# Forming the sums of two weight matrices two chunks after their loads, adding the last product last, and ending the last pair on VectorE

## The chip, the cores and the metric

The kernel runs on one core of one Trainium2 chip. A core has five engines, each with a queue of its own that it works off in order: TensorE (PE, matmuls; PEld is its weight load), VectorE (DVE), ScalarE (ACT), GpSimd (POOL) and SyncE (SP, which here only issues DMAs). An instruction that waits holds up everything behind it in its own queue. The metric is the device time of one execution in microseconds (us), median of several runs.

## What is computed

The reference takes x of shape (8, 1024, 512), normalizes each row to xn, and adds the product of two branches:

```python
x = L0_attn_x
xn = _layernorm(x, axis=-1)
s = _L0_attn_ref(xn, ...)             # four heads of 128 columns, joined by warboss_w
g = _silu(_L0_ffn_ref(xn, w1, b1, w2, b2))
x = x + s * g
...
h = jax.nn.relu(jnp.einsum('bsd,dw->bsw', x, w1) + b1)   # 512 -> 2048
return jnp.einsum('bsw,wd->bsd', h, w2) + b2             # 2048 -> 512
```

The four heads are a full attention ("local"), an attention in which each row keeps its 102 largest scores ("sparse"), a memory head and a small prediction head. All in float32.

## The kernel before

**Tiles.** For each of 8 batches there are 8 tiles of 128 tokens, in 4 pairs of 256 tokens. The feed-forward branch works on groups of 512 tokens (16 of them) for the first matrix, and on pairs (32) for the second.

**Seven products instead of eight.** Both feed-forward matmuls use a 2x2 block scheme with seven products. The weights are cut into 8 "up" chunks (w1) and 8 "down" chunks (w2); a chunk is a tile `w` of seven slots of 128x256. Three slots are loaded as they stand, a fourth raw block `extra` is loaded beside them, and four slots are sums and differences made on the chip: on DVE for "up", on POOL for "down". Slot order is the order in which PE uses them: slots 0 and 1 of a chunk are loaded ones, slot 2 is the first sum. The finished chunk is also written to a DRAM buffer (`w_up_dram`, `w_down_dram`) and loaded from there ready made every later time. So sums are made only for the first 16 chunks of `order_of_chunks`, in the first group: up 0 to 4, then down 0, up 5, down 1, up 6, down 2, up 7, down 3, and down 4 to 7.

`load_chunk` (line 420) does all of it at once: it takes one of four buffers `w`, issues the loads on SP, then the four sums on DVE or POOL, then the write-back on SP. `feed_forward` (541) calls it for chunk at+3 when PE starts chunk at; `first_tokens` (913) calls it for chunks 0 to 2. `extra` shares a ring of three small buffers, `tmp`, with the memory and prediction heads.

**From products to values.** The seven products of an "up" chunk are copied by ACT from PSUM to `u` (or, after the last "down" chunk of a pair, to `m`), two slots to a copy, the seventh alone. `add_products` (454) adds them up in four POOL instructions, of which the second and third need the seventh product (slot 6). `hidden_units` (491) then has ACT make h = relu; `hidden_sums` (507) makes the four token sums `hs` of a "down" chunk on POOL; `make_gate` (526) adds b2 on POOL and has ACT take the Silu. `token_sums` (475) makes the token sums `t` of a group on POOL.

**The end of a pair.** `finish_pair` (823) multiplies the four heads by warboss_w (matmul po), copies to `o` on ACT, adds the bias on POOL, multiplies by the gate on POOL (`o<-o,m`), adds x (`xr<-xr,o`) on POOL and issues the output DMA from POOL's queue.

**Order of the work.** All of it is written out by a planner in the kernel. `clock` holds a planned time for each engine in columns; `run` (132) picks the first chain of work whose due time has come, by rank, and fills PE's remaining time with the feed-forward matmuls (`filler`). Each helper adds its cost (`on_pool`: 60 + 1.42 columns an element; `on_dve`: 340) and yields a due time. `InOrder` (77) ties every instruction to the one before it on its engine, so that the queues have exactly this order, and makes L85 the line of nearly every instruction in the profile; groups are told apart by their tile names. Selection on DVE is a chain of rounds (`sparse_select`, 687): MAX8 finds the eight largest of a row and MATCH_REPLACE8 strikes them out, 13 rounds a tile. `prepare_stats` (863) loads rows of the next batch as `xs` for their mean and variance; the Sqrt is ACT's (`sd<-ve`).

Names in the profile: ph, f, po, pa, sc, ptp are matmul results (up products, down products, joined heads, attention, scores, transposed probabilities); el and es are the local and sparse exponentials; x_up and x_down are the raw blocks.

Of the kernel before, what the change touches and what calls it, by code (L numbers as in the profile page):

```python
# [15 lines left out]
P = 128  # L16
# [4 lines left out]
def kernel(  # L21
# [163 lines left out]
    def on_dve(op, out, in0, in1):  # L185
        getattr(dve, op)(out, in0, in1)
        on("dve", 340)
# [229 lines left out]
    def halves(ap):  # L417
        return ap.rearrange("p (c n) -> p c n", c=2)

    def load_chunk(at):  # L420
        if at >= len(order_of_chunks):
            return
        kind, n, k = order_of_chunks[at]
        w = sb.tile([P, 7, H], F32, tag="w", name=f"w_{kind}_{n}_{k}", bufs=4)
        w_tiles[kind, n, k] = w
        if n:
            sp.dma_start(out=w, in_=w_dram[kind, k])
            return
        extra = sb.tile([P, H], F32, tag="tmp", name=f"x_{kind}_{k}", bufs=3)
        if kind == "up":  # L430
            for slot, u, h in ((0, 0, 0), (1, 0, 1), (4, 1, 1)):
                sp.dma_start(out=halves(w[:, slot]), in_=w1v[:, h, :, u, k])
            sp.dma_start(out=halves(extra), in_=w1v[:, 0, :, 1, k])
            on_dve("tensor_add", w[:, 5], extra, w[:, 4])
            on_dve("tensor_sub", w[:, 2], w[:, 5], w[:, 0])
            on_dve("tensor_sub", w[:, 3], w[:, 0], extra)
            on_dve("tensor_sub", w[:, 6], w[:, 1], w[:, 2])
        else:
            for slot, h, d in ((0, 0, 0), (1, 1, 0), (6, 1, 1)):
                sp.dma_start(out=w[:, slot], in_=w2v[:, h, k, ts(d, H)])  # L440
            sp.dma_start(out=extra, in_=w2v[:, 0, k, H:])
            on_pool("tensor_sub", w[:, 5], extra, w[:, 0])
            on_pool("tensor_sub", w[:, 2], w[:, 6], w[:, 5])
            on_pool("tensor_sub", w[:, 3], w[:, 6], extra)
            on_pool("tensor_sub", w[:, 4], w[:, 1], w[:, 2])
        sp.dma_start(out=w_dram[kind, k], in_=w)
# [4 lines left out]
    def twice(ap):  # L451
        return ap.unsqueeze(1).to_broadcast([P, 2, H])

    def add_products(m):

        for to, add in (
            (m[:, 1:3], twice(m[:, 0])),
            (m[:, 3:7:3], twice(m[:, 2])),
            (m[:, 6], m[:, 5]),
            (m[:, 4:6], twice(m[:, 3])),  # L460
        ):
            on_pool("tensor_add", to, to, add)
            yield


# [23 lines left out]
        tokens[g] = (b11, b21, t[:, 1], t[:, 2], t[:, 3], t[:, 0], b22)  # L489

    def hidden_units(g, k, m):
        for _ in add_products(m):
            yield pool_is_free
        yield after("pool")
        for j, slots in enumerate(((1, 4), (6, 5))):
            h = sb.tile([P, 2, T], F32, tag=f"h{j}", name=f"h_{2 * g + j}_{k}", bufs=(5, NWC)[j])
            for u in range(2):
                act.activation(h[:, u], m[:, slots[u]], AF.Relu, bias=bcol(k + NWC * u))
                on("act", 280)
            hidden[2 * g + j, k] = h  # L500
        units_made[0] += 1
# [21 lines left out]

    wanted_at = {}

    def make_gate(n, m):
        for _ in add_products(m):
            yield pool_is_free
        gs = [m[:, 1:7:5], m[:, 4:6]]
        for g in gs:  # L530
            on_pool("tensor_add", g, g, b2.rearrange("p (h n) -> p h n", h=2))
            yield pool_is_free
        yield after("pool")
        for g in gs:
            act.activation(g, g, AF.Silu)
            on("act", 360)
        b, p = divmod(n, NP)
        gate[b, p] = gs
        done.add(("gate", b, p))

    def feed_forward():

        sums = []
        for at, (kind, n, k) in enumerate(order_of_chunks):
            if kind == "up":
                wants[0] = lambda: (
                    "constants" in done and n in tokens and units_made[0] > n * NWC + k - 2
                )
            else:
                wants[0] = lambda: (n, k) in operands and wanted_at[n, k] <= clock["pe"] and (  # L550
                    k < NWC - 1 or n == 0 or ("gated", *divmod(n - 1, NP)) in done
                )
            yield 0
            if kind == "down":
                wants[0] = lambda: True
            load_chunk(at + 3)
            w = w_tiles.pop((kind, n, k))
            if kind == "up":
                m = sb.tile([P, 7, T], F32, tag="u", name=f"u_{n}_{k}", bufs=2)
            elif k == NWC - 1:  # L560
                m = sb.tile([P, 7, H], F32, tag="m", name=f"m_{n}")
            for i in range(7):
                if kind == "up":
                    if i % 2 == 0:
                        ps = ring(f"ph_{n}_{k}_{i}", (P, 2, T))
                    for c in range(2):
                        pe.matmul(
                            ps[:, i % 2], halves(w[:, i])[:, c], tokens[n][i][:, c],
                            start=c == 0, stop=c == 1,
                        )  # L570
                        yield T
                else:
                    if i % 2 == 0:
                        if k == 0:
                            sums.append(
                                ps_f.tile([P, 2, H], F32, tag="f", name=f"f_{n}_{i}")
                            )
                        ps = sums[i // 2]

                    pe.matmul(  # L580
                        ps[:, i % 2], operands[n, k][i], w[:, i],
                        start=(k == 0 and i % 2 == 0), stop=(k == NWC - 1),
                        skip_group_check=True,
                    )
                    yield H
                if (i % 2 or i == 6) and (kind == "up" or k == NWC - 1):
                    a = i - i % 2
                    copy(m[:, a : i + 1], ps[:, : i + 1 - a], 180 * (i + 1 - a))
            if kind == "up":
                start(hidden_units(n, k, m), rank=0)  # L590
                if k == NWC - 1:
                    tokens.pop(n)
                    done.add(("up", n))
                    if n + 1 < GROUPS:
                        start(token_sums(n + 1), rank=0)
            else:
                operands.pop((n, k))
                downs_made[0] += 1
                if k == NWC - 1:
                    sums = []  # L600
                    start(make_gate(n, m), rank=2)
# [221 lines left out]
    def finish_pair(b, p):  # L823
        yield needs(*[("head", b, p, h) for h in (LOCAL, 2, 3)])
        if (b, p) != (0, 0):
            yield needs(("out", *divmod(b * NP + p - 1, NP)))
        yield can_borrow(2)
        done.add(("borrowed", b, p))
        both = [borrow(f"wb_{b}_{p}_{k}", warboss_w[ts(k, T), :]) for k in range(2)]
        xs = [load_x("xr", b, 2 * p + j, "xr") for j in range(2)]  # L830
        yield clock["pe"] + AHEAD
        yield needs(("head", b, p, SPARSE))
        yield after("act")
        order = (LOCAL, 2, 3, SPARSE)
        os = []
        for j in range(2):
            ps = ring(f"po_{b}_{p}_{j}", (P, D))
            accumulate(
                ps,
                [heads[b, p, h][:, ts(j, P)] for h in order],  # L840
                [both[h // 2][:, h % 2, :] for h in order],
                D,
            )
            o = sb.tile([P, D], F32, tag="o", name=f"o_{b}_{p}_{j}", bufs=2)
            copy(o, ps, 360)
            on_pool("tensor_add", o, o, wb)
            os.append(o)
            yield pool_is_free
        give_back(2)
        done.add(("joined", b, p))  # L850
        yield needs(("gate", b, p))
        yield after("act")
        for j, o in enumerate(os):
            on_pool("tensor_mul", halves(o), halves(o), gate[b, p][j])
            yield pool_is_free
        done.add(("gated", b, p))
        for j, o in enumerate(os):
            on_pool("tensor_add", xs[j], xs[j], o)
            pool.dma_start(out=out[b, ts(2 * p + j, P), :], in_=xs[j])
        done.add(("out", b, p))  # L860


# [50 lines left out]
    def first_tokens():  # L913
# [6 lines left out]
            due += [ln_apply(0, j, first_x[j]) for j in four]  # L920
        for at in range(3):
            load_chunk(at)
        for g in range(NG):
            for j in range(4 * g, 4 * g + 4):
                yield due[j]
# [93 lines left out]
```

## Time and profile before

| | |
|---|---|
| median of 3 runs | 3025.64 us (3025.1 to 3027.43) |
| the profiled execution's own time | 3025.14 us |
| its span, first to last instruction | 3023.4 us |
| mean granted clock of PE | 0.992 of full speed |
| DMA | 488.29 MB, mean 162 GB/s |
| POOL, u<-u of 128x512, 384 times | 1295 ns each |
| POOL, u<-u of 128x256, 128 times | 741 ns each |
| DVE, a selection round (MAX8, MATCH_REPLACE8) | 1228 and 1208 ns |
| DVE waiting for x_up, in total | 34.6 us, 7 times |
| POOL waiting for x_down, in total | 38.7 us, 6 times |
| ACT, a table load, 132 times | 1283 ns each |

Durations are of one profiled execution. Time outside the span (1.7 us here) belongs to the execution but to no instruction. A timeline row gives start, duration, engine, line, operation and tiles; the bracket at its end gives how long the engine had been idle and what ended that. A float32 matmul appears as two passes, so that 7 products with 2 contraction steps are 28 rows.

### The profile page before, as it was taken

Reading aid. Unit: us, or ns where it says so; the run is one execution under the profiler, and the core shown is the slowest. Engines: PE = TensorE matmul, PEld = TensorE weight load, DVE = VectorE, ACT = ScalarE, POOL = GpSimd, SP = SyncE. Lnnn points to the kernel's source line nnn. Section 1 sums busy time; section 2 is a strip of 40 time slices with the busy share of each in tenths; the row PEclk is TensorE's granted clock in tenths of the full one; section 3 lists DMA queues with packets and bytes.
Section 4 is the critical chain, followed back from the end, with each engine's and each line's share of the span. In section 5 each row is a group of like instructions: output and inputs, shape, how many; then the busy total and the mean of one; then the engine's idle time right before and its main releaser. Section 6 shows DMA issues by size and latency. Waiting matters only on the chain.

```text
span 3023.4 us, 36222 instructions
## 1 busy us (share of the span) xinstructions
PE 2937.0 (97%) x12868; PEld 2313.2 (77%) x12868; DVE 2334.8 (77%) x3158; ACT 1550.0 (51%) x2864; POOL 1656.3 (55%) x2097
## 2 busy tenths in 40 slices
PE   7989999999999999999999999999999999999997
PEld 5767877777777877877777877778878777777786
DVE  6878769787698786987679884899839898778760
ACT  3445544555455644555446564465644556355552
POOL 3475645556346653564636555366653655536566
PEclk9999999999999999999999999999999999999999
DMA  6454444455345453454545534445444544535444
GB/s 183 143 205 157 174 131 148 169 186 186 114 139 192 165 185 133 139 194 142 190 134 174 188 131 169 139 167 188 160 157 153 181 160 149 173 108 181 157 162 152
DMA packets 170052, 488.29 MB, mean 162 GB/s; under 512 B 13966, under 2 KB 76448, under 8 KB 169872
## 3 DMA queue, kind: packets, MB, share of 16 engines
q1 hardware_dynamic: 164256, 468.24, 45.6%
q0 software_dynamic: 5616, 17.74, 1.5%
q8 instruction: 102, 1.67, 0.2%
q14 instruction: 78, 0.64, 0.1%
HBM read 454.47 MB, written 31.46 MB: 161 GB/s over the span
## 4 chain that ended last, share of the span: by engine, by line
PE 85%; DVE 5%; ACT 5%; POOL 2%; DMA 2%; issue 1%; SPq 1%; POOLq 0%; DVEq 0%; ACTq 0%
PE f L85 22%; PE ph L85 21%; PE pa L85 7%; PE po L85 7%; PE sc L85 6%; PE pk L85 4%; PE pv L85 4%; PE ptp L85 3%; PE pq L85 3%; DVE top L85 2%; DVE left L85 2%; PE ppi L85 2%; PE pmp L85 2%; PE pp L85 2%; ACT L85 1%; PE pmo L85 1%
## 5 line engine op out<-in xcount | busy, mean ns | idle before, releaser
L85 POOL TENSOR_TENSOR u<-u 128x512 f32<-128x512 f32 (+1 forms) x512 | 591.7, 1157 | 688.8 <-ACT u L85 669.0
L85 DVE MAX8 top<-left 128x8 f32<-128x1024 f32 x768 | 943.2, 1228 | 26.7
L85 DVE MATCH_REPLACE8 left<-top,left 128x1024 f32<-128x1024 f32 x704 | 850.7, 1208 | 0.0
L85 PE MATMUL f<-w_down,hs 128*128 128x256 f32 x2048 | 542.0, 381 | 2.5 <-ACT m L85 2.2
L85 PE MATMUL ph<-t,w_up 128*128 128x256 f32 x2048 | 487.6, 380 | 2.7 <-ACT u L85 2.4
L85 PEld LDWEIGHTS f<-w_down,hs 128*128 128x128 f32 x2048 | 383.1, 191 | 70.6 <-issue 21.1
L85 PEld LDWEIGHTS ph<-t,w_up 128*128 128x128 f32 x2048 | 383.4, 190 | 66.1 <-issue 15.5
L85 PE MATMUL f<-w_down,h 128*128 128x256 f32 x1536 | 425.3, 382 | 3.6 <-ACT m L85 3.6
L85 PE MATMUL ph<-xnT,w_up 128*128 128x256 f32 x1536 | 389.9, 381 | 0.0
L85 POOL TENSOR_TENSOR hs<-h 128x128 f32<-128x128 f32 x512 | 242.6, 474 | 256.4 <-PE f L85 239.9
L85 ACT COPY u<-ph 128x512 f32<-128x512 f32 (+1 forms) x512 | 264.0, 530 | 167.2 <-PE ph L85 165.8
L85 PEld LDWEIGHTS f<-w_down,h 128*128 128x128 f32 x1536 | 287.6, 191 | 57.2 <-issue 18.1
L85 PEld LDWEIGHTS ph<-xnT,w_up 128*128 128x128 f32 x1536 | 287.4, 191 | 49.7 <-issue 14.7
L85 PE MATMUL sc<-kT,qT 128*128 128x512 f32 x512 | 242.6, 596 | 5.5 <-ACT qT L85 3.2
L85 ACT ACTIVATE h<-u,biasT 128x256 f32<-128x256 f32 x512 | 220.0, 501 | 43.8 <-POOL u L85 43.8
L85 PE MATMUL po<-wb,head 128*128 128x512 f32 x512 | 231.4, 595 | 6.5 <-ACT head L85 6.3
L85 PE MATMUL pa<-pT,v 128*128 128x256 f32 x1024 | 234.4, 383 | 2.4 <-ACT el L85 2.4
L85 PEld LDWEIGHTS pa<-pT,v 128*128 128x128 f32 x1024 | 196.4, 192 | 32.1 <-ACT el L85 3.1
L85 DVE MAX8 top<-s 128x8 f32<-128x1024 f32 x64 | 78.2, 1222 | 164.8 <-ACT s L85 164.7
L85 ACT COPY pT<-ptp 128x512 f32<-128x512 f32 x256 | 149.1, 586 | 96.3 <-PE ptp L85 95.1
L85 POOL TENSOR_TENSOR o<-o,wb 128x512 f32<-128x512 f32 x64 | 81.3, 1271 | 196.5 <-ACT o L85 196.4
L85 POOL TENSOR_TENSOR m<-m 128x512 f32<-128x512 f32 (+1 forms) x128 | 146.9, 1147 | 64.6 <-ACT m L85 60.4
(116 smaller groups left out, 3776.6 us busy)
## 6 DMA issues: line engine op xcount, KB each, us to landing
w_down<-w_down_dram SPq DMA_DIRECT2D x248, 896.0 KB, 4.7
w_up<-w_up_dram SPq DMA_DIRECT2D x120, 896.0 KB, 4.6
wb<-in_L_attn_warboss_w_dram SPq DMA_DIRECT2D x64, 512.0 KB, 6.2
xl<-in_L_attn_x_dram SPq DMA_DIRECT2D x64, 256.0 KB, 4.7
xr<-in_L_attn_x_dram SPq DMA_DIRECT2D x64, 256.0 KB, 3.3
out_dram<-xr POOLq DMA_DIRECT2D x64, 256.0 KB, 3.0
xs<-in_L_attn_x_dram SPq DMA_DIRECT2D x56, 256.0 KB, 4.7
wmp<-_attn_memory_proj_w_dram SPq DMA_DIRECT2D x32, 256.0 KB, 3.0
```

Source lines behind the costliest of these rows:

```text
L85: r = made(*args, **kwargs)
```

## The change

Three things are changed.

1. `load_chunk` keeps only the loads. The sums and the write-back move to a new function `form_chunk`, called for chunk at+1 when PE starts chunk at (where loads are issued for at+3), and once for chunk 0 in `first_tokens`. The raw blocks get seven slices of their own, in the buffer that later holds `m`.
2. `add_products` takes the engine to use, and works in five instructions (two of 512 columns, three of 256) of which only the last needs the seventh product.
3. For the last pair of the last batch, the additions of `make_gate`, the product with the gate and the addition of x are on DVE, and the output DMA is issued on SP. The bias of `o` stays on POOL.

```diff
+    raw = {}
+    raw_blocks = sb.tile([P, 7, H], F32, tag="m", name="raw_blocks")
+
     def load_chunk(at):
...
-        extra = sb.tile([P, H], F32, tag="tmp", name=f"x_{kind}_{k}", bufs=3)
+        extra = raw[kind, k] = raw_blocks[:, at % 7]
         if kind == "up":
             for slot, u, h in ((0, 0, 0), (1, 0, 1), (4, 1, 1)):
                 sp.dma_start(out=halves(w[:, slot]), in_=w1v[:, h, :, u, k])
             sp.dma_start(out=halves(extra), in_=w1v[:, 0, :, 1, k])
+        else:
+            for slot, h, d in ((0, 0, 0), (1, 1, 0), (6, 1, 1)):
+                sp.dma_start(out=w[:, slot], in_=w2v[:, h, k, ts(d, H)])
+            sp.dma_start(out=extra, in_=w2v[:, 0, k, H:])
+
+    def form_chunk(at):
+
+        if at >= len(order_of_chunks) or order_of_chunks[at][1]:
+            return
+        kind, n, k = order_of_chunks[at]
+        w, extra = w_tiles[kind, n, k], raw.pop((kind, k))
+        if kind == "up":
             on_dve("tensor_add", w[:, 5], extra, w[:, 4])
...
-    def add_products(m):
-
-        for to, add in (
+    def add_products(m, add):
+
+        for to, more in (
             (m[:, 1:3], twice(m[:, 0])),
-            (m[:, 3:7:3], twice(m[:, 2])),
-            (m[:, 6], m[:, 5]),
+            (m[:, 3], m[:, 2]),
+            (m[:, 2], m[:, 5]),
             (m[:, 4:6], twice(m[:, 3])),
+            (m[:, 6], m[:, 2]),
         ):
-            on_pool("tensor_add", to, to, add)
+            add("tensor_add", to, to, more)
             yield
...
+    LAST = B * NP - 1
+
     def make_gate(n, m):
-        for _ in add_products(m):
-            yield pool_is_free
+        add, free = (on_dve, lambda: True) if n == LAST else (on_pool, pool_is_free)
+        for _ in add_products(m, add):
+            yield free
...
             load_chunk(at + 3)
+            form_chunk(at + 1)
...
+        late = b * NP + p == LAST
+        op, free = (on_dve, lambda: True) if late else (on_pool, pool_is_free)
         for j, o in enumerate(os):
-            on_pool("tensor_mul", halves(o), halves(o), gate[b, p][j])
-            yield pool_is_free
+            op("tensor_mul", halves(o), halves(o), gate[b, p][j])
+            yield free
         done.add(("gated", b, p))
         for j, o in enumerate(os):
-            on_pool("tensor_add", xs[j], xs[j], o)
-            pool.dma_start(out=out[b, ts(2 * p + j, P), :], in_=xs[j])
+            op("tensor_add", xs[j], xs[j], o)
+            (sp if late else pool).dma_start(out=out[b, ts(2 * p + j, P), :], in_=xs[j])
...
         for at in range(3):
             load_chunk(at)
+        form_chunk(0)
```

More of the change, by code (lines that the diff above doesn't have):

```diff
@@ L438, in load_chunk @@
         else:
-            for slot, h, d in ((0, 0, 0), (1, 1, 0), (6, 1, 1)):
-                sp.dma_start(out=w[:, slot], in_=w2v[:, h, k, ts(d, H)])
-            sp.dma_start(out=extra, in_=w2v[:, 0, k, H:])
             on_pool("tensor_sub", w[:, 5], extra, w[:, 0])
@@ L491, in hidden_units @@
     def hidden_units(g, k, m):
-        for _ in add_products(m):
+        for _ in add_products(m, on_pool):
             yield pool_is_free
@@ L524 @@
     wanted_at = {}
+    LAST = B * NP - 1
     def make_gate(n, m):
-        for _ in add_products(m):
-            yield pool_is_free
+        add, free = (on_dve, lambda: True) if n == LAST else (on_pool, pool_is_free)
+        for _ in add_products(m, add):
+            yield free
         gs = [m[:, 1:7:5], m[:, 4:6]]
         for g in gs:
-            on_pool("tensor_add", g, g, b2.rearrange("p (h n) -> p h n", h=2))
-            yield pool_is_free
-        yield after("pool")
+            add("tensor_add", g, g, halves(b2))
+            yield free
+        yield after("dve" if n == LAST else "pool")
         for g in gs:
@@ L852, in finish_pair @@
         yield after("act")
+        late = b * NP + p == LAST
+        op, free = (on_dve, lambda: True) if late else (on_pool, pool_is_free)
         for j, o in enumerate(os):
-            on_pool("tensor_mul", halves(o), halves(o), gate[b, p][j])
-            yield pool_is_free
+            op("tensor_mul", halves(o), halves(o), gate[b, p][j])
+            yield free
         done.add(("gated", b, p))
         for j, o in enumerate(os):
-            on_pool("tensor_add", xs[j], xs[j], o)
-            pool.dma_start(out=out[b, ts(2 * p + j, P), :], in_=xs[j])
+            op("tensor_add", xs[j], xs[j], o)
+            (sp if late else pool).dma_start(out=out[b, ts(2 * p + j, P), :], in_=xs[j])
         done.add(("out", b, p))
```

## The prediction

> **What bounds the kernel now.** I read the page first, then busy time by stretch, then what the matmul engine (PE) waited for, then the timelines around its longest waits, then the end. A difference of 0.2% (6 us) is about what a measurement of this kernel can tell.
>
> The page gives the frame: one core, PE busy for nearly the whole span.
>
> ```profile
> span 3023.4 us, 36222 instructions
> PE 2937.0 (97%) x12868; PEld 2313.2 (77%) x12868; DVE 2334.8 (77%) x3158; ACT 1550.0 (51%) x2864; POOL 1656.3 (55%) x2097
> ```
>
> So a gain can come only from the 86.4 us in which PE is idle, or from matmuls that run slower than usual. Busy time by stretch (length, then busy time of PE, PEld, DVE, ACT, POOL, then the granted PE clock) says where they are:
>
> ```profile
> 44.00:240.00 196.00, 170.56 (x723) 137.02 (x722) 157.53 (x216) 84.97 (x156) 111.09 (x146) 0.94 0.52 168
> 240.00:2959.00 2719.00, 2689.84 (x11850) 2121.16 (x11850) 2155.37 (x2891) 1438.92 (x2657) 1490.20 (x1872) 1.00 0.47 161
> 2959.00:3005.30 46.30, 46.24 (x200) 36.91 (x198) 1.07 (x4) 13.94 (x27) 32.56 (x49) 1.00 0.53 184
> 3005.30:3023.40 18.10, 0.00 (x0) 0.00 (x0) 0.00 (x0) 1.84 (x3) 9.77 (x9) 0.64 0.08 29
> ```
>
> PE loses 25.4 us in the 196 us in which the weights are made, at a granted clock of 0.94; 29.2 us are spread over the next 2719 us; and 18.1 us come after the last matmul. The rest lies before 44 us, where the change moves nothing that PE waits for.
>
> The waits of PE from 0 to 300 us (in total, times, longest) name ScalarE (ACT) as the last releaser:
>
> ```profile
> PE ptp L85 <- ACT el L85: 6.3, 2, 4.6
> PE po L85 <- ACT head L85: 6.3, 1, 6.3
> PE ptp L85 <- ACT es L85: 6.2, 1, 6.2
> PE pp L85 <- ACT h L85: 3.2, 1, 3.2
> ```
>
> ACT had been held itself. The timelines of DVE and POOL show by whom, the bracket giving idle time and releaser:
>
> ```profile
> 111.28 0.42 DVE L85 TENSOR_TENSOR w_up<-x_up,w_up 128x256 f32<-128x256 f32 x1 [9.97 <-DMA x_up<-in_L_ffn_w_dram]
> ```
> ```profile
> 181.87 0.69 DVE L85 BATCH_NORM_STATS2 st<-xs 128x6 f32<-128x512 f32 x1 [15.08 <-DMA xs<-in_L_attn_x_dram]
> ```
> ```profile
> 164.68 0.73 POOL L85 TENSOR_TENSOR w_down<-x_down,w_down 128x256 f32<-128x256 f32 x1 [7.44 <-DMA x_down<-in_L_ffn_w_dram]
> ```
>
> The four sums of a chunk stand right behind its loads, so DVE or POOL waits 4 to 10 us for the transfer with everything else of that queue behind it; the write-back stands behind the sums on SP, so the next loads and xs wait too: a loop SP, DMA, DVE or POOL, SP. What hangs on it is the softmax: at 206.14 PE waits for es, whose DVE rounds stood still for 15.08 us because xs was queued behind a write-back. At 163 to 172 PE waits for head, whose copy stands on ACT behind the h of a unit whose POOL sums were behind x_down.
>
> A long wait costs more than itself:
>
> ```profile
> 172.27 2.08 PE L85 MATMUL po<-wb,head 128*128 128x512 f32 x2 [6.31 <-ACT head L85]
> ...
> 174.99 1.91 PE L85 MATMUL f<-w_down,h 128*128 128x256 f32 x4
> ...
> 178.69 1.03 PE L85 MATMUL f<-w_down,hs 128*128 128x256 f32 x4
> ```
>
> Four passes of 128x256 take 1.91 us after the wait and 1.03 us later.
>
> [...] The trace has 2.5 to 6.8 us from issue to landing for x_up. [...]
>
> **The change, part by part.**
>
> *Sums behind their loads.* Per chunk 3 loads, the raw block, 4 sums and 1 write-back remain, for 16 chunks. The sums of chunk c are now issued at the start of chunk c-1, two chunks after their loads, and the write-back goes with them, past the 4 loads of chunk c+2 on SP. The shortest "up" chunk is 28 passes of 0.215 us = 6.0 us on PE, so loads have 9 us and more for a landing of 3 to 7 us: DVE and POOL stop waiting for w_up and w_down. The built order bears it out: the sums of chunk 2 now stand behind two selection rounds, and the first MAX8 (48.16 us before, behind 6.18 us of waiting) can start when s is copied, at 42.6.
>
> What can go: the PE idle from 44 to 240 us, 2.02+0.34+4.58+0.17+1.75+3.20+0.31+0.27+6.31+0.28+6.18 = 25.4 us, and half-speed time after the four long ones. From start to start in the PE timeline, against 0.215 us a pass (0.43 for 512 columns, 0.11 for 128), these cost 2.4 (at 62.4), 1.8 (129.2), 2.3 (172.3) and 2.6 us (206.1), 9.1 us. Sum 34.5 us.
>
> What is late next, worked through the order of the changed kernel:
> - The sums have a lead of one chunk. DVE needs 1.5 us for them (0.42 each, starts 0.34 apart; up to 1.4 each beside POOL), PE reads the first sum two products (1.7 us) into the chunk. On POOL 4 x 0.73 = 2.9 us against 3.0 us of PE for a "down" chunk. Following both queues I find them 2 us or more ahead everywhere: nothing, at worst 3 us. The raw blocks leave the three tmp buffers for seven slices of the buffer of m; their last reader, the sums of chunk 15, stands a chunk before the first copy to m: nothing.
> - The last "down" chunk of pair 0: its hs now waits for h, which stands on ACT behind the copy of o, and POOL adds wb (1.27) first. After the last po: 0.6 copy, 1.27, then hs 2 x 0.45: PE waits about 2 us (0 to 3).
> - In the new order ACT has the Sqrt of batch 1's statistics (sd) between the second and third copy of the first m. sd waits for ve on DVE, which has no slack: from the first MAX8 to ve at 204.15 it had 156.0 us, less 30.0 waiting, 126 us; from 42.6, with the sums of two more chunks (3 to 5 us), ve comes at 172 to 176. PE, at 199.96 for the es it waited on, less 27.5 of the losses above that come before it, less 7 "down" products (3.0), plus the 2 us just named, wants the freed sums at 171.5: a wait of 1 to 6 us, 4.5 with the copy; 1 for half-speed. This takes the place of the es wait, which is further on now.
>
> New losses 2+4.5+1 = 7.5; net 27 us.
>
> *Last product added last.* Before: three POOL sums of 512 columns (1.295 us) and one of 256 (0.741), 4.63 us; after: two and three, 4.81. For 128 units and 31 gates 0.18 us each is 29 us on POOL, which idles for 45% of the span. Hidden: POOL works ahead of PE (it waited 669.0 us for ACT to copy u), PE waited for hs 0.3 us in all. Zero, bounds -5 (four sums no longer wait for the last product) and +5; if POOL became the pace it would be the 29 us.
>
> *Last pair's end on DVE.* After the last matmul (3005.28) the chain before is
>
> ```profile
> 3006.00 1.26 POOL L85 TENSOR_TENSOR o<-o,wb 128x512 f32<-128x512 f32 x1 [2.17 <-ACT o L85]
> 3007.22 2.48 POOL L85 TENSOR_TENSOR m<-m,b 128x512 f32<-128x512 f32 x2
> 3009.66 2.48 POOL L85 TENSOR_TENSOR o<-o,m 128x512 f32<-128x512 f32 x2
> 3012.10 1.26 POOL L85 TENSOR_TENSOR xr<-xr,o 128x512 f32<-128x512 f32 x1
> ...
> 3015.83 0.56 POOL L85 DMA_DIRECT2D out_dram<-xr  x1 [0.30 <-POOL xr L85]
> ```
>
> Seven POOL instructions and two issues, the last ending at 3016.4. Now m, its five sums and b2 run on DVE beside the 7 us of po; the Silus too, behind a new table load of 1.28 us (the trace's mean) that fits before the last copy. Left: copy to 3005.9, o+wb on POOL to 3007.26, then on DVE one multiply and two additions at 0.69 us ([...]bounds 0.6 and 0.75) to 3009.4, and SP's issue, 0.34 us. SP has nothing else left. The last issue starts at 3009.5 instead of 3015.83: 6.3 us, and 0.2 for the shorter issue. Landing is taken as equal (SP's xr 2.7 us, POOL's out 2.8; bounds 1 either way). Gain 6.5.
>
> *The reshuffled order.* The planner counts the sums elsewhere and yields once more per unit, so the order of all engines differs to the end. The 29.2 us of small waits between 240 and 2959 will be dealt anew: zero, give or take 6 us.
>
> **Sum.** The profiled execution took 3025.14 us (span 3023.4; the median is 3025.64, 0.5 above). 3025.1 - 27 - 6.5 = 2991.6; I say 2991.
>
> **Rivals.**
> - *DVE becomes the bound of the first 240 us.* For: 157.5 of 196 us busy, and PE cannot pass ve before DVE; sums beside POOL took 1.4 us instead of 0.42 at 57 and 131 us. If DVE loses 12 us more, the first part brings 15: 3025.1 - 15 - 6.5 = 3004. Against: the planner puts PE's needs where DVE is due.
> - *No new wait at all*, since ve comes in time: 34.5 + 6.5, 2984, less with a lucky order.
> - *The order does not loosen the loop*, SP being held on buffers that PE frees: only the end gains, 3018. Against: SP waited for PE 28 us from 40 to 210 us, but each load is now wanted two chunks later.
> - *Slower: POOL paces the middle.* A fifth sum per unit lengthens the way from the last product to h, and hs queues behind it. If 0.4 us shows on PE for each of 128 units, 51 us are lost against 33.5 won: 3043; it decides from 0.26 us a unit. Against: POOL's 0.3 us on PE's list.
>
> **How the numbers follow.** Chances: forecast 0.52, DVE bound 0.20, no new wait 0.12, only the end 0.06, slower 0.10. The range reaches from the no-wait case, less 4 for the order, to the DVE case plus 5: 2980 to 3009. Faster by over 0.2% (below 3019.6): 0.87, from the first three cases and half of the fourth; within 0.2%: 0.04, the rest of the fourth and a little of the last; slower: 0.09.
>
> **What would show it.** DVE's and POOL's waits for x_up and x_down (34.6 and 38.7 us) all but gone; the first MAX8 near 42.6 us; PE idle from 44 to 240 us at 5 to 10 us, at a clock near 0.99; a PE wait for a copy of m near 172 us; POOL busy near 1673 us (29 us of sums more, 12 us less at the end); last issue 4 to 5 us after the last matmul. It would be wrong if PE waited for w_up, w_down or POOL's h in many chunks, or the idle time from 240 us on grew beyond 45 us.

## The result and the profile after

The median went from 3025.97 us (3025.1 to 3027.43, four runs) to 2978.89 us (2975.75 to 2981.37, four runs): a ratio of 0.9842, 95% interval 0.9827 to 0.9856, or 47 us. The forecast of 2991 had the direction right and the gain 12 us too small; the measured median lies 1.1 us below the range of 2980 to 3009. The profiled execution of the changed kernel took 2975.75 us, the shortest of its four and 3.1 us under their median, so 49.4 us are to be explained between the two profiles.

The head of its page, in the same form as before:

```profile
span 2974.0 us, 36408 instructions
PE 2923.6 (98%) x12868; PEld 2304.0 (77%) x12868; DVE 2338.7 (79%) x3169; ACT 1549.2 (52%) x2863; POOL 1686.2 (57%) x2244
```

Busy time by stretch (length, then PE, PEld, DVE, ACT, POOL, the granted PE clock, DMA share, GB/s), cut at this kernel's own last matmul:

```profile
44.00:240.00 196.00, 191.50 (x858) 155.04 (x857) 187.28 (x260) 104.07 (x195) 125.82 (x170) 0.99 0.56 190
240.00:2964.80 2724.80, 2701.57 (x11912) 2130.74 (x11911) 2128.86 (x2860) 1434.06 (x2647) 1546.41 (x2053) 1.00 0.47 162
2964.80:2974.00 9.20, 0.01 (x1) 0.00 (x0) 1.89 (x3) 0.59 (x1) 1.26 (x1) 0.77 0.16 59
```

The idle time of a stretch is its length less the first number in the rest of the row. Set beside the kernel before:

| us of idle PE | before | after | won | forecast |
|---|---|---|---|---|
| first 44 us | 13.7 | 13.5 | 0.2 | 0 |
| 44 to 240 us | 25.4 | 4.5 | 20.9 | 18.9 (25.4 less 2 + 4.5) |
| 240 us to the last matmul | 29.2 | 23.2 | 6.0 | 0, give or take 6 |
| last matmul to the end of the span | 18.1 | 9.2 | 8.9 | 6.5 |
| PE busy, for the same 12868 rows | 2937.0 | 2923.6 | 13.4 | 8.1 (half speed, 9.1 less 1) |
| sum | | | 49.4 | 33.5 |

The same matmuls took 13.4 us less busy time. How much of this is half speed can be read off the granted clock. From 44 us to the last matmul it stands at 0.50 in five stretches of the kernel before and in one of the changed kernel (length, then PE busy first):

```profile
61.18:68.00 6.82, 5.62 (x18) 4.70 (x19) 6.68 (x9) 4.69 (x10) 0.77 (x2) 0.50 0.66 211
129.43:132.84 3.41, 3.41 (x9) 2.70 (x9) 2.61 (x4) 1.33 (x4) 2.25 (x3) 0.50 0.00 0
170.40:177.22 6.82, 4.95 (x10) 3.29 (x11) 0.00 (x0) 3.45 (x6) 4.04 (x6) 0.50 0.35 105
204.54:211.36 6.82, 5.22 (x17) 4.39 (x18) 6.30 (x12) 3.32 (x5) 2.03 (x4) 0.50 0.01 2
2505.12:2511.94 6.82, 5.60 (x13) 4.53 (x14) 5.85 (x6) 2.14 (x4) 0.00 (x0) 0.50 0.11 36
```
```profile
167.35:170.76 3.41, 3.41 (x9) 2.73 (x9) 3.24 (x5) 1.87 (x2) 3.33 (x6) 0.50 0.00 0
```

In the last of these, two passes of 256 columns start 0.85 us after the two before them, against 0.43 elsewhere, so half of the PE time in such a stretch is lost: in the head (44 to 240 us) 9.6 us before and 1.7 after, that is 7.9 won where 8.1 were forecast, and in the middle (240 us to the last matmul) 2.8 and 0. The other 2.7 us are about what fewer interruptions make. PE has 46 waits from 44 us on before and 35 after. By estimate each costs 0.27 us of busy time: four passes take 1.13 us right behind a wait and 1.03 otherwise (at 164.94 and 170.78 us of the changed kernel), and the modelled end of the last pass ahead of it lies 0.17 us behind its share of 0.215 (one pass by itself has 0.38 us in the trace).

Of the 16 us missing in the forecast, 6 are idle time in the middle and 2.8 half speed there, 2.7 the interruptions, 2.4 the end and 2 the head's idle time.

PE's waits of the first 300 us, in the form of before (total, times, longest):

```profile
PE ptx L85 <- DVE xl L85: 9.7, 1, 9.7
PE pk L85 <- ACT xnT L85: 3.7, 2, 3.2
PE f L85 <- ACT m L85: 2.5, 1, 2.5
PE f L85 <- DMA xs<-in_L_attn_x_dram: 1.1, 1, 1.1
PE f L85 <- POOL hs L85: 0.8, 1, 0.8
```

The first two lie before 44 us. The four waits of before (el, head, es and h, 22 us together) are gone; the three last rows are what is left. DVE and POOL no longer wait for a raw block (x_up and x_down, here `raw_blocks`): no such wait is left in their lists of the first 300 us, where before it was 34.6 and 38.7 us. The first selection round starts when s is copied:

```profile
42.44 1.23 DVE L85 MAX8 top<-s 128x8 f32<-128x1024 f32 x1 [17.91 <-ACT s L85]
```

The wait for a copy of m is the one that was forecast. Its chain on DVE, ACT and PE:

```profile
174.22 0.17 DVE L85 TENSOR_SCALAR ve<-mv 128x8 f32<-128x8 f32 x1
```
```profile
169.08 1.28 ACT L85 ACT_TABLE_LOAD   x1
174.42 0.21 ACT L85 ACTIVATE sd<-ve 128x8 f32<-128x8 f32 x1 [4.06 <-DVE ve L85]
174.54 0.84 ACT L85 COPY m<-f 128x512 f32<-128x512 f32 x2
```
```profile
175.16 0.70 PE L85 MATMUL f<-w_down,h 128*128 128x256 f32 x2 [2.49 <-ACT m L85]
```

DVE's rounds reach ve at 174.22; the Sqrt on ACT, behind its table load, has waited 4.06 us for it with the third copy of m behind it; PE waits 2.49 us for the PSUM that this copy frees.

The tail, all engines, from the last copy on:

```profile
2964.91 0.59 ACT L85 COPY o<-po 128x512 f32<-128x512 f32 x1 [0.39 <-PE po L85]
2965.57 1.26 POOL L85 TENSOR_TENSOR o<-o,wb 128x512 f32<-128x512 f32 x1 [2.17 <-ACT o L85]
2966.86 0.69 DVE L85 TENSOR_TENSOR o<-o,m 128x512 f32<-128x512 f32 x1 [2.07 <-POOL o L85]
2967.47 1.28 DVE L85 TENSOR_TENSOR xr<-xr,o 128x512 f32<-128x512 f32 x2
2968.19 0.94 SPq L85 DMA_DIRECT2D out_dram<-xr  x2
```

Both issues are done at 2969.13, 4.3 us after the last matmul, where before it was 11.1 (3016.39 less 3005.30).

### The profile page after: what moved, and what is told of

Same layout as the page of the kernel before. It is cut to its first block, busy times and chain, and to the rows that moved or that the text cites. A ratio compares the mean times of both kernels' runs of the same rounds, so it can differ in the third digit from the quotient of the medians.

```text
span 2974.0 us, 36408 instructions
## 1 busy us (share of the span) xinstructions
PE 2923.6 (98%) x12868; PEld 2304.0 (77%) x12868; DVE 2338.7 (79%) x3169; ACT 1549.2 (52%) x2863; POOL 1686.2 (57%) x2244
## 4 chain that ended last, share of the span: by engine, by line
PE 86%; DVE 7%; ACT 4%; POOL 1%; issue 1%; DMA 1%; SPq 0%; POOLq 0%; DVEq 0%; ACTq 0%
PE f L85 22%; PE ph L85 21%; PE pa L85 7%; PE po L85 7%; PE sc L85 7%; PE pk L85 4%; PE pv L85 4%; PE pq L85 3%; PE ptp L85 3%; DVE top L85 3%; DVE left L85 3%; PE pmp L85 2%; PE pp L85 2%; PE ppi L85 2%; ACT L85 1%; PE pmo L85 1%
## 5 line engine op out<-in xcount | busy, mean ns | idle before, releaser
L85 POOL TENSOR_TENSOR u<-u 128x256 f32<-128x256 f32 (+1 forms) x640 | 619.2, 973 | 478.0 <-ACT u L85 453.4
L85 POOL TENSOR_TENSOR hs<-h 128x128 f32<-128x128 f32 x512 | 249.4, 487 | 374.9 <-PE f L85 362.8
L85 POOL TENSOR_TENSOR m<-m 128x256 f32<-128x256 f32 (+1 forms) x155 | 147.8, 958 | 56.1 <-ACT m L85 50.9
```

Source lines behind the costliest of these rows:

```text
L85: r = made(*args, **kwargs)
```

## The experiments

### The sums right behind their loads again (e1)

```diff
         for at in range(3):
             load_chunk(at)
-        form_chunk(0)
+            form_chunk(at)
...
-            form_chunk(at + 1)
+            form_chunk(at + 3)
```

The raw blocks keep their seven slices, and the other two parts of the change stay.

> Only the first part is undone: sums and write-back stand right behind their loads again (raw blocks keep their own slices, five sums and the VectorE end stay). If the delay of the sums carries the gain of the first part, PE loses 30 to 37 us between 44 and 240 us again, DVE and POOL wait 30 us and more for the raw blocks, and the time is 3000 to 3015 us. Rival, the gain came from the raw blocks leaving the tmp ring: the first part stays as good as in the changed kernel, 2975 to 2985 us.

Measured: 3013.42 us (3012.76 to 3014.66), ratio to the kernel before, measured again beside it (3027.91 us), 0.9954 (0.9939 to 0.9969). Busy time by stretch and PE's waits of the first 300 us:

```profile
44.00:240.00 196.00, 171.17 (x732) 136.34 (x731) 154.66 (x218) 85.70 (x157) 112.91 (x159) 0.95 0.52 169
```
```profile
PE po L85 <- ACT head L85: 6.4, 1, 6.4
PE pp L85 <- ACT hi L85: 4.5, 1, 4.5
...
PE f L85 <- POOL hs L85: 3.8, 1, 3.8
PE ptp L85 <- ACT el L85: 3.3, 2, 2.5
PE ptp L85 <- ACT es L85: 2.9, 1, 2.9
```

DVE waits 35.4 us for the raw blocks again, POOL 44.5, and DVE 15.9 us for xs. The head loses 24.8 us of idle time, at a clock of 0.95, although the raw blocks no longer use the small ring `tmp`: the delay wins the head, not the new place of the raw blocks. (The 30 to 37 us expected are reached only with half speed: PE is busy for 15.9 us of the head at a clock of 0.50, of which 8 are lost.) Undoing the delay costs 34.5 us.

### Four sums with the last product early (e2)

```diff
             (m[:, 1:3], twice(m[:, 0])),
-            (m[:, 3], m[:, 2]),
-            (m[:, 2], m[:, 5]),
+            (m[:, 3:7:3], twice(m[:, 2])),
+            (m[:, 6], m[:, 5]),
             (m[:, 4:6], twice(m[:, 3])),
-            (m[:, 6], m[:, 2]),
```

> Only the second part is undone: four sums per unit, three of them behind the seventh product in the queue. If the second part is worth nothing by itself and merely deals the middle anew, the time is 2979 us give or take 6, with PE idle from 240 us to its last matmul anywhere from 17 to 33 us, and POOL waits for ACT u go back from 453 us to about 670. Rival, adding the last product last shortens waits of PE in the middle: idle there returns to 29 us or more, 2984 to 2990 us.

Measured: 2981.58 us (2981.24 to 2983.82), 2.7 above the changed kernel, with 8.5 us of idle PE in the head instead of 4.5 (its wait for a copy of m is 5.9 us) and 24.8 in the middle. POOL is busy for 1652.7 us instead of 1686.2, so the fifth addition costs it 33 us that PE doesn't see. POOL's group of hs (busy us and mean ns, then POOL's idle time ahead of it and what ended it), first in this run, then in the changed kernel:

```profile
L85 POOL TENSOR_TENSOR hs<-h 128x128 f32<-128x128 f32 x512 | 244.4, 477 | 288.9 <-PE f L85 269.7 <-ACT h L85 19.0
```
```profile
L85 POOL TENSOR_TENSOR hs<-h 128x128 f32<-128x128 f32 x512 | 249.4, 487 | 374.9 <-PE f L85 362.8 <-ACT h L85 11.7
```

With five sums POOL stands at hs, ready, for 363 us in all until PE frees a buffer; with four for 270. Its waits for ACT's copies to u are 453 and 613 us (about 670 were expected). The longer list of sums leaves POOL further ahead; less of it has to wait for the seventh product, which fits. That is the opposite of the slower rival, in which POOL became the pace.

### The last pair on POOL again (e3), and only its output there (e4)

```diff
-    LAST = B * NP - 1
+    LAST = B * NP
```
```diff
-            (sp if late else pool).dma_start(out=out[b, ts(2 * p + j, P), :], in_=xs[j])
+            pool.dma_start(out=out[b, ts(2 * p + j, P), :], in_=xs[j])
```

The first undoes all of the third part, the second only the queue of the output. PE's order stays that of the changed kernel in both.

> Only the third part is undone: the last pair ends on POOL as before; PE has the same order of instructions as in the changed kernel. From the last matmul to the end of the span 18 us instead of 9.2, all else equal: 2979 + 9 = 2988 us. If the end is instead hidden by something that ends later anyway, no more than 2 us slower.

> The last pair is computed on DVE, but its two output DMAs are issued from POOL as all others are. The prediction took the landing as equal; the trace has 7.0 us from the last issue's end to the end of the span with POOL and 4.9 with SP. If the queue makes this difference, the span ends 2 us later than with SP and an issue 0.2 us longer: from the last matmul to the end 11.3 to 11.8 us. If it is chance, 9.2 to 9.8 us.

Measured: e3 2989.37 us (2988.75 to 2992.41), 18.9 us from the last matmul to the end of the span; e4 2981.12 us (2980.06 to 2981.79), 11.9 us. So the end is worth 10.5 us of the medians, and 9.7 us of tail (the stretch from the last matmul to the end of the span). e4 lies just above the 11.3 to 11.8 us expected if the queue makes the difference. The end of e4's timeline, whose span ends at 2978.3:

```profile
2969.06 1.28 DVE L85 TENSOR_TENSOR xr<-xr,o 128x512 f32<-128x512 f32 x2
2970.04 0.56 POOL L85 DMA_DIRECT2D out_dram<-xr  x1 [1.62 <-DVE xr L85]
2970.77 0.54 POOL L85 DMA_DIRECT2D out_dram<-xr  x1 [0.17 <-issue]
```

The last addition ends 0.97 us before the last issue does here, and 0.38 us before it with SP: 0.6 of the 2.7 us. The rest comes after the issue. Both kernels by short stretches around the last traffic, the DMA share being the last number but one:

```profile
2970.00:2971.00 1.00, 0.00 (x0) 0.00 (x0) 0.00 (x0) 0.00 (x0) 0.00 (x0) 0.50 0.41 154
2971.00:2971.50 0.50, 0.00 (x0) 0.00 (x0) 0.00 (x0) 0.00 (x0) 0.00 (x0) 0.50 0.00 0
```
```profile
2972.00:2973.00 1.00, 0.00 (x0) 0.00 (x0) 0.00 (x0) 0.00 (x0) 0.00 (x0) 0.50 0.70 262
2973.00:2973.50 0.50, 0.00 (x0) 0.00 (x0) 0.00 (x0) 0.00 (x0) 0.00 (x0) 0.50 0.00 0
```

The first block is the changed kernel (issue done 2969.13, data moved by about 2970.4, span ends 2974.0), the second e4 (2971.31, about 2972.7, 2978.3). From issue to last data it is 1.3 and 1.4 us, equal as the prediction took it; from last data to the end of the span 3.6 and 5.6 us, in which no engine is busy.

This looks like the work of the queue, but e4 changes something else too: POOL's own last instruction. In the changed kernel that is the bias of `o`, done at 2966.83, 7.2 us before the end of the span; in e4 it is the second issue, done at 2971.31, 7.0 us before it. In all fourteen profiles of this case in which POOL still works after the last matmul, the span ends 6.8 to 7.2 us after POOL's last instruction, whichever queue issues the output (7.0 in the kernel before, 6.9 in e3). In the other four (e7, e8, e11, e12, below) POOL falls silent more than 16 us before the end, and the span ends 3.0 to 3.4 us after SP's last issue. So the end of the span fits the later of two times, POOL's last instruction and some 7 us, or SP's last issue and some 3 us. What happens in the 7 us, the trace doesn't say.

### The same work dealt out otherwise (e5, e6, e9, e10)

```diff
-    SLACK = 400
+    SLACK = 390
```

SLACK is the time that the planner leaves after an instruction before it plans its reader. 390 and 410 change only the order (and with it the number of ACT's table loads: 131, 131 and 129 in the changed kernel at 400, 390 and 410). Such an order is called a dealing here. e5 and e6 are the changed kernel with 390 and 410, e9 and e10 the kernel before.

> The changed kernel with the planner's slack at 390 columns instead of 400: the same sums, waits and engines, dealt out in another order from the first group on. Theory (the 8 us won between 240 us and the last matmul are mostly the luck of one dealing, since no wait that the change touches stands there in number): idle PE between 240 us and the last matmul moves by several us against 23.2, anywhere from 20 to 29, and the median lies between 2974 and 2990. Rival (the five sums and the earlier m copies win them wherever the work lands): 23 +- 1.5 us idle, and the PE waits for a copy of m stay at none; median 2979 +- 2.5. The head (44 to 240 us) should keep its 4 to 9 us under both.

> The changed kernel with the planner's slack at 410 columns instead of 400, a third dealing of the same work. Same two theories: luck of the dealing gives 20 to 29 us of idle PE between 240 us and the last matmul and a median between 2974 and 2990; a lasting gain of the change gives 23 +- 1.5 us and 2979 +- 2.5.

> The kernel before with the planner's slack at 390 columns: none of the change, only another dealing of the same work. Between 240 us and the last matmul PE was idle 29.2 us in the kernel before, and 17.6, 19.5 and 23.2 us in three dealings of the changed kernel. Theory (the middle is the luck of a dealing): here it falls anywhere between 17 and 30, and one of this run and the next at 24 or below. Rival (the change itself takes 6 to 10 us of waits out of the middle): 27 to 32 in both. End 18 us and head about 25 us idle under both. Median 3014 to 3027.

> The kernel before with the planner's slack at 410 columns, a third dealing of it. Luck of the dealing: 17 to 30 us of idle PE between 240 us and the last matmul; lasting gain of the change: 27 to 32. Head about 25, end 18 under both.

Measured: e5 2972.36 us (2971.38 to 2974.5), e6 2974.35 (2973.45 to 2977.69), e9 3024.35 (3022.93 to 3027.78), e10 3020.30 (3018.74 to 3021.44). The middle of e5 and of e9 by stretch:

```profile
240.00:2962.22 2722.22, 2704.65 (x11923) 2133.45 (x11921) 2131.07 (x2863) 1437.26 (x2648) 1544.58 (x2053) 1.00 0.47 162
```
```profile
240.00:3004.42 2764.42, 2735.53 (x12042) 2158.30 (x12040) 2165.96 (x2892) 1450.98 (x2682) 1521.09 (x1920) 1.00 0.47 161
```

17.6 us idle in the one, 28.9 in the other. Neither theory holds as it was written. A dealing alone moves the middle by up to 5.6 us (23.2, 17.6, 19.5 for the changed kernel), so the 23 +- 1.5 of the second fails; but both new values also lie below the 20 to 29 of the first. The kernel before has 29.2, 28.9 and 25.7: no dealing at 24 or below, against luck alone, and one below the 27 to 32 of a lasting gain. The scatter belongs to the order and not to the single execution: e3, e4 and e7 have PE's order of the changed kernel row for row and leave 23.0, 22.6 and 22.5 us idle against its 23.2; e11 has that of e5, 17.5 against 17.6. At equal slack the change is worth 47.1, 52.0 and 46.0 us.

### Which part wins the middle (e13 to e16)

e13 and e14 are the kernel of e2, e15 and e16 that of e1, each at slack 390 and 410.

> The changed kernel with the four sums of before in add_products, slack 390. At slack 400 it left PE idle for 24.8 us between 240 us and the last matmul. If the delay of the weight sums carries the middle's gain, about 20 (17 to 24) here, as with five sums; if the five sums carry it, 26 to 29.

> As the run before, slack 410. Delay carries it: 17 to 24 us idle in the middle. Five sums carry it: 26 to 29.

> The changed kernel with the weight sums right behind their loads again, slack 390; five sums and VectorE end stay. At slack 400 it left PE idle for 27.8 us in the middle. If the five sums carry the middle's gain, 17 to 24 us here; if the delay carries it, 26 to 29. Head about 25 us, end 8.9 under both.

> As the run before, slack 410. Five sums carry it: 17 to 24 us idle in the middle. Delay carries it: 26 to 29.

Measured, with the earlier runs; idle PE from 240 us to the last matmul, and the median, at slack 400, 390 and 410:

| | idle in the middle | mean | median |
|---|---|---|---|
| before | 29.2, 28.9, 25.7 | 27.9 | 3025.97, 3024.35, 3020.30 |
| five sums, no delay, end on DVE | 27.8, 34.0, 22.8 | 28.2 | 3013.42, 3021.87, 3006.47 |
| delay, four sums, end on DVE | 24.8, 25.6, 30.2 | 26.9 | 2981.58, 2982.86, 2990.60 |
| all three parts | 23.2, 17.6, 19.5 | 20.1 | 2978.89, 2972.36, 2974.35 |

(The medians of e13 and e14 are of two runs, that of e16 of three.) Neither part alone moves the mean; both together do, by 8 us. But a row scatters by as much as 11 us, and three dealings of each are few; a fourth with all three parts, e12 below, which also moves a Sqrt, leaves 23.7. That the changed kernel's middle is shorter than that of before is likely; that it takes both parts is what these numbers look like, and no mechanism for it was shown. The experiment misses its aim: at 390 neither part gives its gain by itself (25.6 and 34.0), and at 410 e16 (22.8) and e14 (30.2) point to the five sums, which e1 and e15 contradict.

It does correct two sizes. Undoing the delay costs 34.5, 49.5 and 32.1 us at equal slack, undoing the fifth sum 2.7, 10.5 and 16.3. A part measured at one dealing is worth what that dealing makes of it. One piece of the fifth sum's gain is steady, and it stands in the head: without it PE is idle there for 8.5, 8.5 and 10.1 us, with it for 4.5, 5.2 and 6.2, a difference of 3.3 to 4.0 us. Why was not traced.

### One more step of the end on VectorE, and the Sqrt later (e7, e8)

```diff
-            copy(o, ps, 360)
-            on_pool("tensor_add", o, o, wb)
+            if late:
+                on_dve("tensor_add", o, ps, wb)
+            else:
+                copy(o, ps, 360)
+                on_pool("tensor_add", o, o, wb)
```

e8 adds to this

```diff
+        yield clock["pe"] + 4000
         ln_rstd(b, 0, NT)
         done.add(("rstd", b))
```

> The changed kernel with one more step of the last pair on VectorE: the bias is added straight from PSUM on VectorE, in place of the ScalarE copy and the POOL addition; PE's order is the changed kernel's but for the interleaving of the last pair. Theory (the tail is the sum of this chain: copy 0.6, POOL 1.26, then 0.69 each for product and addition): the stretch from the last matmul to the end of the span falls from 9.2 us to about 7.7 and the median from 2978.9 to about 2977.4. Rival (the tail is set by the Silus of the gate, whose table load stands at 2962.1 and whose second ends near 2965.7, or by the landing of the output): 8.7 us or more, median unchanged within 0.7.

> The kernel of the run before (bias of the last pair on VectorE) with the Sqrt of the next batch's statistics planned 4000 columns later, so that it stands on ScalarE behind all four copies of the first m instead of between the second and third. Theory (the wait for that Sqrt is what is left of the head's loss): PE's wait for a copy of m near 172 us goes (2.5 us in the changed kernel's profile, up to 4.2 in other runs with the same start), idle PE from 44 to 240 us falls from 4.5 to 2 to 3 us, and the median by 2 to 4 us against the run before, as far as the new dealing behind it allows (+-4). Rival (another wait stands right behind it, since VectorE is late with the rounds of the sparse head anyway): the idle time stays at 4 to 6 us, with es or el as the releaser.

Measured: e7 2977.56 us (2974.68 to 2978.93), e8 2975.45 (2973.27 to 2976.27). The tail of e7 (last matmul done 2967.95, span ends 2974.9):

```profile
2968.05 0.69 DVE L85 TENSOR_TENSOR o<-po,wb 128x512 f32<-128x512 f32 x1 [2.75 <-PE po L85]
2968.66 1.28 DVE L85 TENSOR_TENSOR o<-o,m 128x512 f32<-128x512 f32 x2
2969.86 1.29 DVE L85 TENSOR_TENSOR xr<-xr,o 128x512 f32<-128x512 f32 x2
2970.57 0.95 SPq L85 DMA_DIRECT2D out_dram<-xr  x2
```

6.95 us instead of 9.2, more than the theory's 7.7. An addition that reads PSUM takes 0.69 us on DVE here, as long as the multiplication of `o` and `m` in SBUF in the changed kernel (0.69 us, tail above), but both products now stand behind it: the last issue is done 3.6 us after the last matmul instead of 4.3, which is 0.7 of the 2.2 us. The other 1.5 us come after the last data. POOL has no work left in this tail; its last instruction stands 19 us before the end of the span:

```profile
2955.29 0.45 POOL L85 TENSOR_TENSOR hs<-h,hs 128x128 f32<-128x128 f32 x1
```

From the end of SP's last issue to the end of the span it is now 3.4 us, where the changed kernel has 4.9. Of the gain of 2.2 us the median shows 1.3, inside the spread of the runs. In e8 PE's waits from 44 to 240 us are

```profile
PE f L85 <- DMA xs<-in_L_attn_x_dram: 1.1, 1, 1.1
PE f L85 <- POOL hs L85: 0.8, 1, 0.8
PE ptp L85 <- ACT es L85: 0.4, 1, 0.4
PE pv L85 <- ACT u L85: 0.2, 1, 0.2
```

The wait for a copy of m is gone and 2.4 us of idle time are left (e7: 6.2). So the Sqrt between two copies of m was the cause of that wait; only 0.4 us for es took its place. The median is 2.1 us under that of e7, which is no more than the spread of the runs.

### Both with the better dealing (e11, e12)

e11 is e7 at slack 390, e12 is e8 at slack 390.

> The changed kernel with slack 390 and the bias of the last pair on VectorE straight from PSUM. If the two gains stand in different places and add up, the median lies 2 us under the run with slack 390 alone (2972.4), at 2970.4, with 7.0 us from the last matmul to the end of the span instead of 8.9; if the tail's gain is lost again, at 2972 or more.

> The run before with the Sqrt of the next batch's statistics 4000 columns later as well, which deals the order anew behind it. If the wait it takes out (3.2 us with slack 390) is a gain of its own, idle PE from 44 to 240 us is 2 to 3 us instead of 5.2 and the median 2967 to 2968 with an equal middle; the middle may move it by 4 us either way.

Measured: e11 2972.63 us (2969.3 to 2974.0), e12 2970.00 (2968.97 to 2972.84), ratio to before 0.9814 (0.9801 to 0.9828). Both miss their forecasts of 2970.4 and 2967 to 2968 by about 2 us. e11's tail is 6.9 us as expected, but its median is that of e5: its wait for a copy of m was 4.2 us in the profile against e5's 3.2, and the tail's gain is lost in such differences of the head. e12's head has 2.3 us left as expected, but its order is another one behind the moved Sqrt, and its middle is 23.7 where e5 had 17.6. Its runs all lie under those of the changed kernel, by 9 us in the medians.

## Where the prediction held, and which steps failed

Undoing one part at a time costs 34.5 us for the delay, 2.7 for the fifth sum and 10.5 for the end, 47.7 together against 47 for the whole; the forecast had 27, 0 and 6.5. The mechanism of the first and largest part held, and the 12 us are missing in the terms below.

**The middle: the step that failed.** "The 29.2 us of small waits between 240 and 2959 will be dealt anew: zero, give or take 6 us." The 6 us are about what a dealing moves; the zero was wrong. Between the profiles it was 6.0 us of idle time and 2.8 of half speed, over half of what was missing. Three dealings of before average 27.9 us of idle time, three of the changed kernel 20.1. Why is open.

**The head: right in mechanism, gain a little too small.** The net 27 us were 18.9 of idle time and 8.1 of half speed. Idle time gave 20.9: the two new losses before hs and h were 1.84 us together (forecast 2; the profile puts one of them down to a DMA of xs, in e2 and e6 to ACT's h), the wait for the copy of m 2.49 (forecast 4.5). That wait is 2.5 us in the profile of the changed kernel and 4.2 in three others with the same order (e3, e4, e7), so 4.5 was near the common value, and part of the gain above the forecast is this one execution. Two sums behind the 4.5 are off. The losses that come before 199.96 add up to 25.7 us by the prediction's own list (19.2 of waits, 6.5 of half speed), not 27.5, so that PE wants the freed sums at 173.3 and not at 171.5; the trace has 172.67. And 126 us from 42.6 with 3 to 5 more are 171.6 to 173.6, not 172 to 176; ve came at 174.22. The new waits were named one by one, which held.

**Half speed: right in size, wrong in place.** The head won 7.9 us against 8.1. But the 1 us kept for the new wait for m is not there in the profiled execution: that wait of 2.49 us has no half speed behind it. The 1.7 us lost lie at 167 to 171 us, behind two short waits, which the prediction left out of its count (last section). The rest of the 13.4 us of busy time, half speed in the middle and fewer interruptions, had no term.

**The second part: zero, bounds -5 and +5.** The fifth sum is hidden on POOL, as the prediction said, and POOL was busy for 1686 us where 1673 were forecast. But at equal slack the second part won 2.7, 10.5 and 16.3 us; two of the three lie beyond the -5. 3.3 to 4.0 us of it are won in the head at every slack; the rest goes with the middle. The reason given for zero, "PE waited for hs 0.3 us in all", did not carry.

**The end: issue right, the path to the end of the span wrong.** The last issue ended 4.3 us after the last matmul (forecast 4 to 5), a gain of 6.8 where 6.5 were forecast. The 0.69 us that the forecast took for each DVE step of 512 columns was not shown by the profile of before, which has no such addition on DVE; in the changed kernel the two products took 0.692 us each and the two additions of x 0.684. "Landing is taken as equal", with 1 us either way, was 2.1 us off. The transfer is equal; what the step missed is that the span ends some 7 us after POOL's last instruction in both kernels. That instruction moved from 11.1 us after the last matmul to 2.0, 9.1 us sooner, and the tail became 8.9 us shorter.

**The rivals.** DVE did not become the bound, but it came near: it was busy for 187.3 of the 196 us and waited for no weights, and the longest wait of PE left in the head hangs on its ve. That wait cost 2.5 to 4.2 us and not 12. The slower rival, POOL as the pace, found the opposite, POOL further ahead. The order did loosen the loop. "No new wait at all" (2984) lies nearer to the result, but a new wait was there; what brought the time down was the rest.

## What to carry to other kernels

Where loads and the work on them are issued together from in-order queues, a step between the load and its first reader can be worth more than the waits it removes: here the head won 20.9 us of idle time and 7.9 of half speed with it, and undoing the delay alone cost 32 to 50 us, the dealing included. In a kernel whose order a planner deals out, measure a part of a change at two or three settings of the planner: one setting put the fifth sum at 2.7 us, the next at 16.3. At the end of a kernel, look not only at the path to the last byte but at what each engine does last: here the tail was shortest, 6.5 to 7.0 us, where POOL had no work in it at all.

## What the runs showed that was not expected

**The span ends about 7 us after POOL's last instruction, whichever queue issues the output.** It is 6.8 to 7.2 us in fourteen profiles; where POOL is silent early, the span ends 3.0 to 3.4 us after SP's last issue. Up to the last data SP and POOL are nearly equal (1.3 and 1.4 us from the end of the issue, in the changed kernel and e4); the difference behind it (3.6 and 5.6 us) goes with POOL's last instruction. No run was made to tell POOL's end from other causes, so this is a reading of the eighteen profiles, not a mechanism shown.

**Where half speed begins.** The prediction counted it behind the four long waits of the head (3.20, 4.58, 6.18 and 6.31 us). In three kernels with all parts of the change the same place had waits of 2.49, 3.22 and 4.23 us (the changed kernel, e5 and e6). After 2.49 the first two passes took 0.70 us and the four passes of scores that follow 1.88, full speed. After 3.22, in e5:

```profile
175.53 0.70 PE L85 MATMUL f<-w_down,h 128*128 128x256 f32 x2 [3.22 <-ACT m L85]
176.06 2.93 PE L85 MATMUL sc<-kT,qT 128*128 128x512 f32 x4
178.79 1.71 PE L85 MATMUL f<-w_down,hs 128*128 128x256 f32 x4
180.34 1.03 PE L85 MATMUL f<-w_down,h 128*128 128x256 f32 x4
```

2.93 and 1.71 us where 1.88 and 1.03 are full speed: about 1.7 us more, and beginning 0.5 us after the wait. After 4.23, in e6, the first two passes already took 1.22 us and the scores 2.99. In the middle of the kernel before, 16 passes of 256 columns took 6.46 us, against 3.4 at the usual 0.215, after a wait of only 2.27 us that another of 1.02 stood close ahead of:

```profile
2503.41 0.66 PE L85 MATMUL ptx<-ident,xl 128*128 128x128 f32 x4 [1.02 <-ACT h L85]
2506.34 6.46 PE L85 MATMUL pa<-pT,v 128*128 128x256 f32 x16 [2.27 <-ACT el L85]
```

And the half speed at 167.35 to 170.76 in the changed kernel follows waits of only 1.08 and 0.76 us, with 1.1 us of work between them. So the length of the last wait does not tell: 2.49 us had no half speed behind it, 2.27 and 0.76 had, each with another wait (1.02 and 1.08 us) close ahead. What does decide was not tested. The stretch in the middle cost about 3 us, more than the wait. Counting half speed only behind single waits of 3.20 us and more, as the prediction did, leaves such places out.
